# Layer 0 of the first two groups ahead of the branch, the search in 16 parts on two engines, and weights of layers 2 and 3 prepared in a later stage

## The chip, the cores and the metric

The kernel runs on one core of one Trainium2 chip. The metric is the device time of one execution in microseconds; of several executions the median is given. The profile is one execution, recorded by the hardware profiler.

## What is computed

Four graph layers follow each other on x (128 batches of 128 tokens by 128 features) with one adjacency of 128 x 128 integers per batch. Before each layer stands h = relu(layernorm(x)), after it x = x + layer(h).

```python
# layer 0
for r in range(1, 8):
    mask = (adj == r); degree = clip(mask.sum(2), 1e-6)
    agg += ((mask / degree) @ h) @ rel_weights[r]
out = relu(layernorm(agg + h @ self_w.T + self_b) * gamma + beta)
# layer 1
D = abs(h[:, :, None, :] - h[:, None, :, :])     # all pairs of tokens
s = leaky(batchnorm(D @ W1.T + b1)) @ W2 + b2    # one score per pair
A = softmax(where(adj > 0, s, -9e15))
y = leaky(batchnorm((A @ h) @ Wg.T + bg)); out = [h, y] @ Wt.T + bt
# layers 2 and 3: graph attention with weights W_2, b_2, a_2 and W_3, a_3
```

The inputs hold an adjacency of zeros and ones only, so relations 2 to 7 never occur. The kernel doesn't assume that: it looks for the highest number in the adjacency and branches on it.

## The kernel before

**Groups and tiles.** The 128 batches are taken in groups of four (G = 4, so 32 groups, NG). A group's x, adj, mask and so on are tiles of 128 x 512. Each batch's pairs are cut into four tiles of 128 x 2048 (NT = 4), 512 tiles in all.

**Start (to L559).** Two groups (AHEAD = 2) begin layer 0 in the generators `layer0(g)`, which run up to `po` (L346 to L351) and stop there, since they lack the sum over the other relations. Beside them `highest` (L274) takes the whole adjacency (8 MB) through VectorE in eight parts of 1 MB, four loaded over ScalarE's queue and four over SP's, through four buffers, and forms `flag` (L391). Then the weights of layers 2 and 3 are prepared (L394 to L467: transposes, products, squares against a bound, a split of the bias into three bf16 pieces), the weights of layer 1 are loaded (L469 on), and the constant `both_t` is made (L505).

**Branch (L512 to L561).** With a flag the other relations are computed for all groups and put into AGG. Without one (`cmp.Else()`, the arm that runs here) the self bias is copied into AGG: two tiles on the chip for groups 0 and 1, and two DRAM tensors `a` of 1.5 and 6 MB for the other 30 groups, by two DMAs on SP (L559). Then both generators finish layer 0 of groups 0 and 1: add, layernorm, gamma and beta, add to x, store to X[g], moments, and H1[g] on ScalarE.

**The pairs stage (to L799).** All further work of layer 0 and of the pairs is a list of `step`s: a name, an engine, a cost, the steps it waits for, a rank and the code. `features` (xp, xe, again, pw, xw) prepares two batches, `pairs` has per tile the difference `d` (L585, tiles 1 and 3 of four on GpSimd, the others on VectorE), `abs` (L624, ScalarE), `hp` (L595, L598, TensorE), `hs` (L608, ScalarE) and `st` (L615, VectorE), and `chain(g)` is layer 0 of group g from 2 on (load, mask, mv, deg, rs, most, per, hn, share, pt, hT, ... o, mvo, rso, oc, on, end, x, mvx, rsx, h1). The load of a group (L685 to L687) is three DMAs on SP: x, adj, and its AGG, into two buffers each.

`_ordered` makes one order of these steps. It keeps a free time per engine and a done time per step; the step with the earliest possible start goes next, the rank decides among equal starts only. A step that waits for names that are not in the list counts as ready at time 0. A step on SP is done LANDING = 3.0 us after its cost:

```python
        done[name] = start + cost + (LANDING if engine == "SP" else 0)
```

The emission runs in a region in which each engine issues its instructions in the order in which they are written (`tc.manual_schedule()`). Instructions outside of such regions are ordered by the compiler, by readiness.

**Layer 1's second half (to L1080).** One slot per batch turns stored pair products into scores; `chain(g)` puts softmax and products of a group into slots 4g + 5 to 4g + 16 by `at(slot, place, work)`. In a slot the places come in the order am, e, p, a, l, s. The last batch has slot 127; in slots 128 to 140 only chains of the last groups are left. Then comes the branch on `bounded` (L1093), with layers 2 and 3 in its arm.

Of the kernel before, what the change touches and what calls it, by code (L numbers as in the profile page):

```python
# [17 lines left out]
P = 128  # L18
G = 4
# [13 lines left out]
AHEAD = 2  # L33
FETCHED = 10
# [132 lines left out]
def tile_gnn_stack(ctx: ExitStack, tc: tile.TileContext, a: dict, out: bass.AP):  # L167
# [89 lines left out]
    with tc.tile_pool(name="c0", bufs=1) as c0, tc.tile_pool(name="p0", bufs=2) as p0:  # L257

        both = c0.tile([P, 2, P], F32, name="both")
        nc.sync.dma_start(both[:, 0, :], a["rel_w"][1])  # L260
        nc.sync.dma_start(both[:, 1, :], a["self_wT"])
# [6 lines left out]

        AGG = [c0.tile([P, G, P], F32, name=f"agg{g}") for g in range(AHEAD)] + AGG
# [5 lines left out]

        def highest(sc):

            n = NB * P // 8
            tops = sc.tile([P, 8], F32, name="tops")
            flat = a["adj"].rearrange("b t s -> b (t s)").rearrange("b (c n) -> c b n", c=8)  # L280
            for c in range(8):
                part = sc.tile([P, n], I32, name="part", bufs=4)
                (nc.scalar if c < 4 else nc.sync).dma_start(part, flat[c])
                nc.vector.tensor_reduce(tops[:, c:c + 1], part, AX.X, OP.max)
            top = sc.tile([P, 1], F32, name="top")
            nc.vector.tensor_reduce(top, tops, AX.X, OP.max)
            pt = sm("ptop")
            nc.tensor.transpose(pt[0:1, 0, :], top, ident)
            nc.vector.tensor_reduce(top[0:1, :], pt[0:1, 0, :], AX.X, OP.max)
            return top[0:1, :]  # L290
# [8 lines left out]
        def act_norm(dst, src, rs, nb):  # L299

            for k in range(G):
                nc.scalar.activation(dst[:, k, :], src[:, k, :], AF.Relu, bias=nb[:, k:k + 1],
                                     scale=rs[:, k:k + 1])
# [4 lines left out]

        def layer0(g):
            bs = slice(g * G, g * G + G)  # L310
            x = p0.tile([P, G, P], F32, name="x")
            nc.sync.dma_start(x, a["x"][bs].rearrange("b t c -> t b c"))
            adj = p0.tile([P, G, P], I32, name="adj")
            nc.sync.dma_start(adj, a["adj"][bs].rearrange("b t s -> t b s"))
            yield
            mv = small.tile([P, G, 2], F32, name="lnmv")
            rs = small.tile([P, G], F32, name="lnrs")
            norm_stats(x, mv, rs)
            nb = shift(mv, rs)
            yield  # L320

            mask = p0.tile([P, G, P], F32, name="mask")
            nc.gpsimd.tensor_scalar(mask, adj, 1, None, op0=OP.is_equal)
            deg = small.tile([P, G], F32, name="deg")
            nc.vector.tensor_reduce(deg, mask, AX.X, OP.add)
            nc.vector.tensor_scalar(deg, deg, 1e-6, None, op0=OP.max)
            nc.vector.reciprocal(deg, deg)
            yield
            h = p0.tile([P, G, P], F32, name="hn")
            act_norm(h, x, rs, nb)  # L330
            nc.gpsimd.tensor_tensor(mask, mask, deg[:, :, None].to_broadcast([P, G, P]), OP.mult)
            nc.gpsimd.tensor_scalar(M8[g], adj, 0, None, op0=OP.is_gt)
            yield
            hT = p0.tile([P, G, P], F32, name="hT")
            transpose(hT, h)
            yield
            maskT = p0.tile([P, G, P], F32, name="maskT")
            transpose(maskT, mask)
            yield
            o = p0.tile([P, G, P], F32, name="o")  # L340
            hw = p0.tile([P, G, P], F32, name="hw")
            ph = sm("ph")
            for k in range(G):
                nc.tensor.matmul(ph[:, k, :], hT[:, k, :], both[:, 0, :], start=True, stop=True)
            nc.scalar.copy(hw, ph)
            yield  # L346
            po = sm("po")
            for k in range(G):
                nc.tensor.matmul(po[:, k, :], hT[:, k, :], both[:, 1, :], start=True, stop=False)
                nc.tensor.matmul(po[:, k, :], maskT[:, k, :], hw[:, k, :], start=False, stop=True)  # L350
            nc.vector.tensor_copy(o, po)  # L351
            yield "rest"
            nc.vector.tensor_tensor(o, o, AGG[g], OP.add)
            yield
            mv = small.tile([P, G, 2], F32, name="lnmv")
            rs = small.tile([P, G], F32, name="lnrs")
            norm_stats(o, mv, rs)
            yield
            for k in range(G):
                nc.vector.scalar_tensor_tensor(o[:, k, :], o[:, k, :], mv[:, k, 0:1], gamma,  # L360
                                               op0=OP.subtract, op1=OP.mult)
            yield
            on = sm("on")
            for k in range(G):
                nc.vector.scalar_tensor_tensor(on[:, k, :], o[:, k, :], rs[:, k:k + 1], beta,
                                               op0=OP.mult, op1=OP.add)
            nc.vector.scalar_tensor_tensor(x, on, 0.0, x, op0=OP.max, op1=OP.add)
            nc.sync.dma_start(X[g], x)
            yield
            norm_stats(x, MV1[:, g], RS1[:, g])  # L370
            nb = shift(MV1[:, g], RS1[:, g])
            yield
            H1[g] = p0.tile([P, G, P], F32, name="h1", bufs=3)
            act_norm(H1[g], x, RS1[:, g], nb)


        H1 = {}
        first = [layer0(g) for g in range(AHEAD)]
        for w in first:
            next(w)  # L380
        with tc.tile_pool(name="sc", bufs=1) as sc:
            top = highest(sc)
            flag = const.tile([1, 1], I32, name="flag")
            for t, v in ((gamma, "gamma"), (beta, "beta")):
                nc.vector.tensor_copy(t, load(v, [P, P], _bcast(a[v], P), pool=c0))
            for k in range(G):
                nc.sync.dma_start(selfb[:, k, :], _bcast(a["self_b"], P))
            for w in first:
                while next(w) != "rest":
                    pass  # L390
            nc.vector.tensor_scalar(flag, top, 1.5, None, op0=OP.is_gt)  # L391

        with tc.tile_pool(name="sw", bufs=1) as sw:


            w2x = const.tile([P, P + 8], F32, name="w2x")
            nc.sync.dma_start(w2x[:, 0:P], a["W_2"])
            w3x = const.tile([P, P + 2], F32, name="w3x")
            nc.sync.dma_start(w3x[:, 0:P], a["W_3"])
            b_2 = load("b_2", [P, P], _bcast(a["b_2"], P))  # L400
            b_2c = col("b_2c", a["b_2"])
            wtyT = load("wtyT", [P, P], a["WtT"][P:2 * P])
            a2 = const.tile([P, 2, 4], F32, name="a2")
            nc.vector.memset(a2, 0.0)
            a3 = const.tile([P, 2, 1], F32, name="a3")
            for part in range(2):
                for hd in range(4):

                    nc.sync.dma_start(a2[32 * hd:32 * hd + 32, part, hd:hd + 1], a["a_2"][32 * (1 - part):][0:32])
                nc.sync.dma_start(a3[:, part, :], a["a_3"][P * (1 - part):][0:P])  # L410
            add_b = sw.tile([P, 8], F32, name="add_b")
            bounds = sw.tile([P, 3, 8], F32, name="bounds")
            nc.vector.memset(bounds, 0.0)
            square = sw.tile([P, 10], F32, name="square")
            for wx, av, n in ((w2x, a2, 4), (w3x, a3, 1)):
                pt = sm("pwt")
                nc.tensor.transpose(pt[:, 0, :], wx[:, 0:P], ident)
                wt = sw.tile([P, P], F32, name=f"wt{n}")
                nc.scalar.copy(wt, pt[:, 0, :])
                pv = sm("pwa")  # L420
                nc.tensor.matmul(pv[:, 0, 0:2 * n], wt, av.rearrange("p a b -> p (a b)"), start=True, stop=True)
                nc.vector.tensor_copy(wx[:, P:], pv[:, 0, 0:2 * n])
                nc.vector.tensor_tensor(square[:, 0:2 * n], wx[:, P:], wx[:, P:], OP.mult)
                pn = sm("pn")
                nc.tensor.matmul(pn[:, 0, 0:2 * n], ones, square[:, 0:2 * n], start=True, stop=True)
                nc.vector.tensor_copy(bounds[:, 0 if n == 4 else 1, 0:2 * n], pn[:, 0, 0:2 * n])
# [82 lines left out]
        for hh in range(2):  # L509
            nc.vector.tensor_tensor(fold[:, hh, :], ident[:, 0:64], ident[:, 64:128], OP.add)  # L510
# [1059 lines left out]
```

## Time and profile before

| | |
|---|---|
| median of 3 runs | 2887.32 us (2887.09 to 2894.89) |
| the profiled execution | 2891.87 us, of which its span 2889.8 |
| mean granted TensorE clock | 0.952 |
| busy: TensorE, VectorE, ScalarE, GpSimd | 85%, 87%, 83%, 60% |
| start, up to the first difference of pairs | 0 to 80 us |
| pairs stage | 80 to about 1600 us |
| layer 1's second half | about 1610 to 2411 us |
| layers 2 and 3 | 2414 us to the end |

How to read it: times are from the span's start. In the timeline a line is start, duration, engine, line of the kernel, operation, output and input tile and how often it comes in a row; in brackets stands how long the engine was idle before, and who ended that. A `q` behind an engine's name is its instruction queue, where DMAs are issued. In the chain of waits each line is a link of the path that ended last.

### The profile page before, as it was taken

To read this page: it belongs to the slowest core of one execution; us is meant where nothing else is said; L and a number is where in the kernel's file an instruction comes from. 1 tells how busy PE (TensorE), PEld (TensorE's weight loads), DVE (VectorE), ACT (ScalarE), POOL (GpSimd) and SP (SyncE) were. 2 spreads that over 40 slices of the span, in tenths; PEclk is the share of its full clock that TensorE was granted. 3 is DMA by queue.
4 is the path that set the end of the run, shared out by engine and by line. 5 is a ranking of instruction groups with operands and counts; after the bars stand their busy time and mean duration, and the time that the engine had idled before them with its cause. 6 is when DMAs were issued, how large, how long until landed. Compare 5 with 4: busy or idle time off the path is not lost.

```text
span 2889.8 us, 41921 instructions
## 1 busy us (share of the span) xinstructions
PE 2469.7 (85%) x14517; PEld 1185.7 (41%) x14517; DVE 2520.0 (87%) x4949; ACT 2392.2 (83%) x2811; POOL 1729.1 (60%) x1613
## 2 busy tenths in 40 slices
PE   1899899999898989898989688888888886998897
PEld 1333333333333333333333234444444444777675
DVE  5799999999999999999999578888888885987886
ACT  1799998989899999999999678777877774988886
POOL 2899989898989899898988001101111104665552
PEclk8899999999999999999999899999999997999998
DMA  5555545454544444454544999999999971111210
GB/s 200 201 202 221 204 190 204 190 204 190 204 193 200 195 199 200 193 207 186 215 171 204 368 408 408 410 409 409 410 410 410 408 283 54 45 59 63 63 34 27
DMA packets 180083, 653.83 MB, mean 226 GB/s; under 512 B 30992, under 2 KB 99472, under 8 KB 129680
## 3 DMA queue, kind: packets, MB, share of 16 engines
q1 hardware_dynamic: 179280, 646.80, 56.3%
q10 hardware_dynamic: 576, 4.19, 0.4%
q8 instruction: 119, 1.95, 0.3%
q14 instruction: 108, 0.88, 0.1%
HBM read 338.14 MB, written 312.80 MB: 225 GB/s over the span
## 4 chain that ended last, share of the span: by engine, by line
PE 36%; ACT 23%; DMA 20%; DVE 12%; issue 5%; POOL 3%; SPq 0%; DVEq 0%; ACTq 0%; POOLq 0%
PE hp L595 17%; ACT d L624 11%; DMA z<-hp 7%; DMA rows<-sk 7%; PE hp L598 5%; ACT hs L608 5%; DMA u<-rows 5%; DVE d L585 3%; PE pv L1292 2%; ACT o L717 2%; PE ps L919 1%; ACT h L1176 1%; DVE z L962 1%; PE po L741 1%; POOL rs L221 1%
## 5 line engine op out<-in xcount | busy, mean ns | idle before, releaser
L585 POOL TENSOR_TENSOR d<-xe 128x2048 f32<-128x2048 f32 x256 | 1074.0, 4201 | 86.2 <-PE hp L595 65.7
L595 PE MATMUL hp<-d,w1T 128*64 128x512 f32 x4096 | 1019.2, 621 | 123.1 <-ACT d L624 65.4
L624 ACT ACTIVATE d<-d 128x2048 f32<-128x2048 f32 x384 | 730.9, 1922 | 9.2 <-POOL d L585 5.0
L585 DVE TENSOR_TENSOR d<-xe,xp 128x2048 f32<-128x2048 f32 x256 | 579.9, 2265 | 28.6 <-PE xp L660 21.2
L608 ACT COPY hs<-hp 128x1024 f32<-128x1024 f32 x512 | 512.1, 1017 | 80.2 <-PE hp L598 43.3
L595 PEld LDWEIGHTS hp<-d,w1T 128*64 128x64 f32 x4096 | 290.9, 142 | 691.7 <-issue 465.3
L1008 POOL TENSOR_TENSOR x<-x,bt 128x512 f32<-128x512 f32 x32 | 43.7, 1366 | 684.7 <-DMA x<-x 684.7
L615 DVE BATCH_NORM_STATS2 st<-hs 128x6 f32<-128x512 f32 x512 | 348.8, 681 | 51.6 <-ACT hs L608 51.6
L616 DVE BATCH_NORM_STATS2 st<-hs 128x6 f32<-128x512 f32 (+1 forms) x512 | 328.7, 642 | 0.0
L962 DVE SCALAR_TENSOR_TENSOR z<-z 128x2048 f32<-128x2048 f32 x128 | 297.0, 2320 | 22.8 <-ACT z L944 22.8
L944 ACT ACTIVATE z<-z,bias,scale 128x2048 f32<-128x2048 f32 x128 | 267.3, 2088 | 18.8 <-DMA z<-hp 18.8
L948 ACT ACTIVATE zr<-z,bias,scale 128x2048 f32<-128x2048 f32 x128 | 267.4, 2089 | 9.7 <-DMA z<-hp 7.5
L598 PE MATMUL hp<-both_t,xw 128*64 128x512 f32 x1024 | 266.2, 594 | 0.0
L919 PE MATMUL ps<-z,w2z 128*32 128x512 f32 x1024 | 141.7, 626 | 83.2 <-DVE z L962 83.2
L926 PEld LDWEIGHTS pk<-pick,su 128*128 128x128 f32 x1024 | 125.7, 193 | 139.9 <-DVE su L940 103.0
L926 PE MATMUL pk<-pick,su 128*128 128x16 f32 x1024 | 138.2, 267 | 25.8 <-DVE su L940 24.7
L1292 PE MATMUL pv<-wr,e 128*128 128x128 f32 x1024 | 148.4, 293 | 10.7 <-DVE e L1269 6.1
L1292 PEld LDWEIGHTS pv<-wr,e 128*128 128x128 f32 x1024 | 133.8, 204 | 19.7 <-issue 3.8
L919 PE MATMUL ps<-z,w2l 128*32 128x512 f32 x1024 | 139.1, 612 | 0.6 <-DMA z<-hp 0.6
L919 PE MATMUL ps<-zr,w2r 128*32 128x512 f32 x1024 | 139.0, 615 | 0.4 <-ACT zr L948 0.4
L598 PEld LDWEIGHTS hp<-both_t,xw 128*64 128x64 f32 x1024 | 78.1, 138 | 143.1 <-issue 142.5
L1269 DVE SCALAR_TENSOR_TENSOR e<-e,ps 128x512 f32<-128x512 f32 x160 | 106.8, 678 | 28.7 <-ACT ps L1266 27.9
(266 smaller groups left out, 3855.5 us busy)
## 6 DMA issues: line engine op xcount, KB each, us to landing
hp<-hs SPq DMA_DIRECT2D x128, 2048.0 KB, 6.3
z<-hp SPq DMA_DIRECT2D x256, 1024.0 KB, 14.8
x<-x SPq DMA_DIRECT2D x128, 256.0 KB, 4.8
u<-rows SPq DMA_DIRECT2D x32, 384.0 KB, 11.6
x<-in_x_dram SPq DMA_DIRECT2D x32, 256.0 KB, 3.0
adj<-in_adj_dram SPq DMA_DIRECT2D x32, 256.0 KB, 3.4
out_dram<-x SPq DMA_DIRECT2D x32, 256.0 KB, 2.5
agg<-a SPq DMA_DIRECT2D x30, 256.0 KB, 3.8
```

What stands on the lines that cost most here:

```text
L585: eng.tensor_tensor(d, ahead, x[:, None, None, :].to_broadcast([P, 2, KC, P]), OP.max if t == BY_MAX else OP.subtract)
L595: nc.tensor.matmul(hp[64 * hh:64 * hh + 64, c:c + 512], w1T2 if by_max else w1T, d[:, hh, c:c + 512], start=True, stop=not by_max, skip_gr ...
L598: nc.tensor.matmul(hp[64 * hh:64 * hh + 64, c:c + 512], XW[i // NT // 2][:, i // NT % 2, :], both_t.rearrange("p h k i -> p h (k i)")[:, h ...
L608: nc.scalar.copy(halves[b][:, t, :], linear.pop(i))
L615: nc.vector.bn_stats(st[:, 2 * t, :], hs[:, 0:512])
L616: nc.vector.bn_stats(st[:, 2 * t + 1, :], hs[:, 512:1024 - P * last])
L624: nc.scalar.activation(diffs[i], diffs[i], AF.Abs)
L919: nc.tensor.matmul(ps[32 * c:32 * c + 32, :], w[:, w0:w0 + 32], v[:, 512 * c:512 * c + 512], start=j0 == 0, stop=w is w2r, skip_group_chec ...
L944: nc.scalar.activation(z0, z0, AF.Identity, bias=bias1, scale=scale1[:, 0:1])
L948: nc.scalar.activation(zr, z1, AF.Relu, bias=bias1, scale=scale1[:, 0:1])
L962: nc.vector.scalar_tensor_tensor(z0, z0, 0.01, z0, op0=OP.mult, op1=OP.max)
L1292: nc.tensor.matmul(t[pv][:, k % 2, hd, :], t[e][:, hd, :], flat[:, at:at + P], start=True, stop=True)
```

## The change

`layer0` and `highest` are gone. The functions `difference` to `features` and `chain` stand earlier in the code, otherwise as they were, but for three things: `chain` takes an `agg` that is already on the chip, its step `ph` waits for `first_loads` too, and its step `on` for `banks`. The start is now a list of steps with its own `_ordered` plan: layer 0 of groups 0 and 1 whole, with the self bias as `agg`, and the search, in 16 parts of 0.5 MB through eight buffers, all loaded on SP, even parts by a maximum on VectorE and odd ones by a sum of relu(adj - 1) on ScalarE.

```diff
-        first = [layer0(g) for g in range(AHEAD)]
...
+        step("first_loads", "SP", 3.0, [("load", AHEAD - 1)], 0, first_loads)
+        step("second_loads", "SP", 1.5, [("part", PARTS // 2 - 1)], 0, second_loads)
+        for c in range(PARTS):
+            step(("part", c), "SP", 1.25 * 16 / PARTS,
+                 ["first_loads"] if c == 0 else [("part", c - 1)] + [("top", c - PARTS // 2)] * (c >= PARTS // 2)
+                 + ["second_loads"] * (c == PARTS // 2), 1, lambda c=c: part(c))
+            step(("top", c), "ACT" if c % 2 else "DVE", 1.2 * 16 / PARTS, [("part", c)], -99, lambda c=c: highest(c))
+        step("top", "DVE", 0.4, [("top", c) for c in range(PARTS)], -99, highest_of_all)
+        step("ptop", "PE", 0.3, ["top"], -99, one_row, takes=("sm",))
+        step("flag", "DVE", 0.4, ["ptop"], -99, flagged, gives=("sm",))
+        step("banks", "ACT", 0.6, ["second_loads"], -40, in_banks)
+        step("both_t", "DVE", 2.6, ["second_loads"], 99, both_tokens)
+        step("fold", "Pool", 0.5, [], 99, folds)
+        for g in range(AHEAD):
+            chain(g, selfb)
+        with tc.manual_schedule():
+            for work in _ordered(steps, {"sm": 2}):
+                work()
```

`first_loads` holds self bias (four DMAs) and both weights of layer 0, `second_loads` gamma, beta and w1T; `banks` copies gamma and beta into PSUM; `both_t` makes w1T2, turns and both_t.

In the branch, the arm with a flag runs `chain(g, o)` for groups 0 and 1 once more with the true sum; the other arm only has the two DMAs into `a`. Behind the branch, the load of group 2 is taken out of the plan and issued first, outside of the hand-written order, and about 30 loads of weights of layers 1 to 3 follow it:

```diff
+        next(s for s in steps if s[0] == ("load", AHEAD))[-1]()
+        steps[:] = [s for s in steps if s[0] != ("load", AHEAD)]
+        b1 = col("b1", a["b1"], 64)
...
+        w2x = const.tile([P, P + 8], F32, name="w2x")
+        nc.sync.dma_start(w2x[:, 0:P], a["W_2"])
...
+                nc.sync.dma_start(a2[32 * hd:32 * hd + 32, part, hd:hd + 1], a["a_2"][32 * (1 - part):][0:32])
```

The preparation of the weights of layers 2 and 3 becomes `brief()`, placed into the last slots of layer 1's second half (end = NB + 1 = 129), behind the chains' own jobs of the same place:

```diff
+            at(end, "a", scratch)
+            at(end, "p", transposed)
+            at(end + 1, "am", copied)
+            at(end + 1, "p", products)
+            at(end + 2, "l", squares)
+            at(end + 3, "p", sums)
+            at(end + 4, "l", compared)
+            at(end + 1, "l", joined)
+            for n in range(3):
+                at(end + 5 + n, "l", lambda n=n: piece(n))
+            at(end + 8, "l", owners)
```

`pick` is now one copy on GpSimd instead of sixteen on VectorE, `fold` is made on GpSimd, and some memsets moved there.

## The prediction

> **What bounds the kernel now.** I read the slices first, then the timeline and the DMA issues of the first 110 us, then the chain at the end of layer 1. Of the 40 slices (72.2 us each) only a few show a hungry TensorE: the first, and the stretch around the seam of layers 1 and 2. The change touches these two places.
>
> ```profile
> PE   1899899999898989898989688888888886998897
> PEclk8899999999999999999999899999999997999998
> DMA  5555545454544444454544999999999971111210
> ```
>
> In the first slice TensorE is busy one tenth: all engines wait for the branch (L512). Its timeline:
>
> ```profile
> 24.27 2.29 DVE L284 TENSOR_REDUCE tops<-part 128x1 f32<-128x2048 int32 x1 [6.76 <-DMA part<-in_adj_dram]
> ...
> 41.45 0.14 DVE L391 TENSOR_SCALAR flag<-top 1x1 int32<-1x1 f32 x1
> ...
> 60.80 1.30 SPq L559 DMA_DIRECT2D a<-selfb  x2
> ...
> 71.56 5.29 SPq L368 DMA_DIRECT2D x<-x  x2
> ...
> 80.41 8.34 POOL L585 TENSOR_TENSOR d<-xe 128x2048 f32<-128x2048 f32 x2
> 81.24 2.29 DVE L585 TENSOR_TENSOR d<-xe,xp 128x2048 f32<-128x2048 f32 x1 [6.25 <-PE xp L660]
> ...
> 84.33 0.40 SPq L685 DMA_DIRECT2D x<-in_x_dram  x1
> ...
> 87.18 0.87 DVE L694 BATCH_NORM_STATS2 lnst<-x 128x6 f32<-128x128 f32 x4 [1.02 <-DMA x<-in_x_dram]
> ```
>
> The flag is there at 41.6, weights work keeps the branch until 58.2 (SP), the rest of layer 0 of groups 0 and 1 fills 63 to 80, and the first differences `d` start at 80.4 (GpSimd) and 81.2 (VectorE). From there about 3 us a tile. The DMA issues of that window, size and median time to landing:
>
> ```profile
> a<-selfb SPq DMA_DIRECT2D x1, 6144.0 KB, 21.7
> ...
> x<-x SPq DMA_DIRECT2D x2, 256.0 KB, 11.0
> ```
>
> The second line is the one to keep: X[0]'s store, issued at 71.56, let the load behind it go only at 84.2, just after the 6 MB of `a` had landed (61.6 + 21.7 = 83.3). Small transfers issued on SP behind that write end with it.
>
> **What the Trainium skill says.** "DMA: Bandwidth & Descriptors", section "Queues, rings and completion order": SP owns one ring on each of the DMA engines and descriptors are consumed in ring order; the 11.0 us of the stores agree (all issues of that name have a median of 4.8 over the run). "TensorE: Matmul & The Clock Gate", section "What's actually happening": half clock after idling, full after sustained work; the trace has a granted clock of 0.50 from 58 to 84 us and 0.58 from 80 to 90, so both kernels enter the pairs cold. "Runtime: NRT & Kernel Launch", section "Instruction fetch mechanics": a taken branch out of the fetched window stalls; here SP needed 2.6 us from branch (58.2) to first DMA (60.8).
>
> **The change, part by part.**
>
> *Search.* `part(c)` names `part(c-1)` as predecessor, and the planner adds LANDING 3.0 to every SP step; so it spaces the parts 1.25 + 3.0 = 4.25 apart: part 7 due at 41.2, the second loads at 45.4, parts 8 and 9 at 49.9 and 54.2. `both_t` and `banks` wait for the second loads (49.9), so `end(0)` is due at 53.9 and the store X[0] at 55.4: ahead of part 10. X[1] (59.7) comes ahead of part 11. A queue is in order: parts 10 to 15 can't leave before layer 0 of these groups is stored. In before the manual orders were kept literally (VectorE ran d, d, mv(2), mv(3), d, as planned), so I take this one literally too.
>
> *Layer 0 of groups 0, 1, ahead of the flag.* x lands at about 4 (3.0 from issue). GpSimd paces it: mask 1.50, roots with shift 1.95, `most` 0.2, m8 1.50, share 1.04 a group: share(0) at 10.9, share(1) at 17.2. Then transposes 0.6, maskT 0.6, `ph` 1.1, hw 0.6, `po` 1.9: `po(1)` ends at 22.6; o 0.7 and moments 1.2: 24.6; roots 1.95: 26.6; centring 1.65: 28.3. ScalarE has top 3, 5, 7 queued next (1.1 each, from 1.92 for twice the elements and 1.02 for a copy of this size) and `banks` 0.55: 32.1. VectorE meanwhile did top 2, 4, 6 (1.14, half of 2.28) and both_t 2.8. on(0) 1.35 and end(0) 0.68: 34.1; top 8 1.14, moments 1.16, on(1), end(1): 38.4. Then SP sends X[1] and parts 11 to 15. A lone 1 MB part took 5.2, of which 2.6 is transfer at 400 GB/s; a half one is 3.9, the store 0.65, each further part 1.3: part 15 at 39.0 + 0.65 + 3.9 + 5.2 = 48.7. top 15 1.1, closing steps 1.2 as before: flag at about **51**. That is 9 later than before, but with nothing left in front of the branch.
>
> *Branch.* Flag read 0.7 and branch 2.6: the `a` writes leave at 54.4 instead of 60.8.
>
> *Load of group 2, moved behind them.* `load(AHEAD)` is taken from the plan, so the planner holds mv(2) and mask(2) ready at time 0 and puts them first on VectorE and GpSimd, ahead of `again(0)`, `d(1)`, `deg(2)`, `d(0)`. Queued behind them is the whole pair work. Their x lands 84.2 - 60.8 = 23.4 after the write's issue: 77.8, adj 0.65 later: 78.5. mask 1.5, `again` 0.3: d(1) at 80.4. deg 0.67: d(0) at 80.8. Against 80.4 and 81.2: **-0.2**. The 26 us that the earlier layer 0 would give are spent in this wait; `features` (xp, xe, pw, xw, some 2 us) hides in it.
>
> *Ramp.* Before, mv(2), mv(3), mask(2), deg(2) stood between the first differences, with waits of 1.0 and 2.6 for x; d(6) began at 95.98. Now only mv(3) does, and its x, issued after the weights, lands near 85. d(6) follows hp(2), near 94: **-2**. The 30 weight DMAs (0.43 each, 13 us of SP) lie in SP's idle time, as `out(0)` is not due until 20 us into the pairs; with that cover gone they cost 13.
>
> *Weights for layers 2, 3 in the tail.* The removed 7.6 us (51.6 to 59.2) lay before the branch and are counted above. `brief` runs in slots 129 to 137, where the last two groups go alone:
>
> ```profile
> 2397.22 0.70 DVE e L1016
> 2398.01 0.70 DVE e L1017
> 2398.73 0.70 DVE mx L1022
> 2399.45 0.70 DVE e L1023
> 2400.18 0.64 ACT e L1062
> 2400.84 0.70 DVE sums L1027
> ```
>
> This chain has no gaps, so what stands between its links costs in full: transposes and b_2c product on PE in slot 129 0.9, `joined` 0.3 (slot 130), `squares` 0.6 (131), `piece` 0 and 1 0.75 each (134, 135) by the durations of L417 to L441. What falls in slots 132, 133, 136, 137 meets an idle VectorE. **+3.3**; between +1 (if PE's and half of VectorE's hide) and +6 (if the three more `sm` banks make a product wait).
>
> *Small edits.* `pick` in one GpSimd copy, `fold` on GpSimd, memsets: under 1 us each, hidden by the search.
>
> Sum: -0.2 - 2 + 3.3 = **+1.1**. Against the profiled execution: 2891.87 + 1.1 = 2893.0; it lies 4.55 above the median, so the median goes from 2887.32 to about **2888**. Unknown: ScalarE's accumulating Relu on int32 is not in the trace; at 0.9 to 1.5 the seven of them that count move the flag by -1 to +3. Own range of this case 2882 to 2895.
>
> **Rivals.**
>
> *Loads leave ahead of the branch (faster).* Work not in a hand-written order can move up a queue: SP's own read of `bounded`, written far below, ran ahead of its branch.
>
> ```profile
> L512 SPq COMPARE_BRANCH  x1: 50/50/50, 58.2 to 58.2; - x1
> ```
>
> ```profile
> L1093 SPq TENSOR_LOAD <-bounded x1: 285/285/285, 57.6 to 57.6; - x1
> ```
>
> x's first buffer is free at about 41. If x and adj of group 2 go then, VectorE starts d(0) near 57, but mv(3) comes third, and its x still ends with the `a` write, at 78.5: d(4) ends at 82 instead of 94.3, so -12.4 + 3.3: **2878**. If group 3's go too, d(0) at 57 instead of 81.2, -24 + 3.3 and most of the ramp's 2: **2867**. Against it: the branch's other arm uses the same buffers, and must find them free.
>
> *Flag later (slower).* From 51 on each us of flag is a us of time, since wait and write hang on it. The 30 weight loads wait for nothing; if they sit on SP ahead of parts 10 to 15, after X[0] or X[1], instead of in the gap before part 8, they add 13 us there, less 2 to 3 by loads gone from the ramp: **2898**. It decides from a flag after 59. For it: w3x needed 5.0 us of SP[...].
>
> **How the numbers follow.** As forecast 0.45; group 2 early 0.15; groups 2 and 3 early 0.17; flag later 0.23. About 0.3% (8.7 us) is what a measurement can tell from no change. Faster: 0.17, half of the 2878 case, 0.05 of the forecast's spread: 0.30. Slower: 0.21 of the late flag and 0.03: 0.24. Same: 0.46. The range 2866 to 2899 takes in the rivals' values and leaves out their outer halves, below 0.2.
>
> **What would show it.** Right: X[1]'s store ahead of part 11 on SP; flag at 48 to 55; VectorE's first work after the branch is moments of x with a wait near 20 us on DMA x; d(1) near 80; the tail after the last `ps` longer by 2 to 4. Wrong: x of group 2 issued before the branch; a flag before 40 (stores not in front of parts) or after 59; parts spread by weight loads.

## The result and the profile after

| | before | after |
|---|---|---|
| median | 2888.2 us (2887.09 to 2894.89, 4 runs) | 2893.7 us (2890.22 to 2897.68, 4 runs) |
| ratio after / before, 95% interval | | 1.0017, 1.0000 to 1.0034 |
| profiled execution, its span, TensorE clock | 2891.87, 2889.8, 0.952 | 2892.36, 2890.5, 0.946 |

The time hardly moved, and what difference there is lies on the slow side. Layer 0 of two groups and the weights of layers 2 and 3 are no longer behind the search, and nothing came of it. In the slices of the page after, the first one is a little fuller for TensorE, 2 in place of 1, and the second, in which the pairs begin, is emptier, 6 in place of 8.

```profile
PE   2699998989898999898989688888888886998897
PEclk7899999999999999999999799999999997999998
DMA  6445444444445454544444899999999971111210
```

The timeline of the kernel after, from the flag to the third pair of differences (start, duration, engine, line, operation; in brackets the idle time before it and who ended it):

```profile
54.68 0.14 DVE L562 TENSOR_SCALAR flag<-top 1x1 int32<-1x1 f32 x1
...
58.99 1.74 SPq L659 DMA_DIRECT2D a<-selfb  x2
61.54 12.48 SPq L700 DMA_DIRECT2D a<-in_a_dram  x1
...
75.41 1.18 SPq L411 DMA_DIRECT2D agg<-a  x1
76.69 1.19 SPq L408 DMA_DIRECT2D x<-in_x_dram  x1
82.69 0.37 SPq L409 DMA_DIRECT2D adj<-in_adj_dram  x1
...
84.79 0.87 DVE L420 BATCH_NORM_STATS2 lnst<-x 128x6 f32<-128x128 f32 x4 [29.97 <-DMA x<-in_x_dram]
86.45 1.50 POOL L430 TENSOR_SCALAR mask<-adj 128x512 f32<-128x512 int32 x1 [41.42 <-DMA adj<-in_adj_dram]
88.27 8.33 POOL L308 TENSOR_TENSOR d<-xe 128x2048 f32<-128x2048 f32 x2
88.59 4.48 DVE L308 TENSOR_TENSOR d<-xe,xp 128x2048 f32<-128x2048 f32 x2
96.14 2.29 DVE L308 TENSOR_TENSOR d<-xe,xp 128x2048 f32<-128x2048 f32 x1 [2.02 <-PE hp L318]
```

Four things are to be seen. VectorE and GpSimd stand still for 30 and 41 us (the first part of that is still the wait for the flag and the branch), and what ends both waits is the load of group 2. That load isn't late by its own size: SP sends x 17.7 us after the first of the two writes of `a`. Right behind the writes stands a load of 128 bytes for a_2, in whose issue SP is held for 12.48 us. And adj leaves 6 us after x, because SP waits before it. The DMA issues of the first 110 us have the write, and the waits of SP have that wait (who waited, for what, us in total, how often, longest):

```profile
a<-selfb SPq DMA_DIRECT2D x1, 6144.0 KB, 22.9
...
x<-in_x_dram SPq DMA_DIRECT2D x4, 256.0 KB, 4.1
```

```profile
SPq L409 <- DMA a<-selfb: 4.8, 1, 4.8
```

The 6 MB write, issued at 59.74, had landed at 82.6, and adj (L409) left at 82.69. So the write holds the load of group 2 in two ways: x by its place in the queue, adj by a wait for the write's landing.

Cut at marks that both kernels have, the spans differ so (in brackets the mark in the trace after):

| stretch | before | after | difference |
|---|---|---|---|
| to the first `d` on GpSimd (88.27) | 80.41 | 88.27 | +7.86 |
| to the end of the pairs stage, the memset of `zero` (1611.77) | 1527.52 | 1523.50 | -4.02 |
| to the end of the last product `ps` (2379.15) | 768.55 | 767.38 | -1.17 |
| to the moments at the seam of layers 1 and 2 (2416.14) | 34.76 | 36.99 | +2.23 |
| layers 2 and 3, to the end | 478.56 | 474.36 | -4.20 |
| sum | 2889.8 | 2890.5 | +0.7 |

The last row is not laid to the change: the code of that stage is the same in all kernels, the ten kernels below took between 472.7 and 477.7 there, and from 120 to 240 us after the seam the granted clock was 0.94 and 0.91 (60 us each) in the profiled execution before, 0.97 in both after. The first, second and fourth rows make +6.1, and the medians differ by 5.5.

### The profile page after: what moved, and what is told of

Read it like the earlier page. It is cut to its first block, busy times and chain, and to the rows that moved or that the text cites. A ratio compares the mean times of both kernels' runs of the same rounds, so it can differ in the third digit from the quotient of the medians.

```text
span 2890.5 us, 41926 instructions
## 1 busy us (share of the span) xinstructions
PE 2472.1 (86%) x14515; PEld 1187.6 (41%) x14515; DVE 2504.7 (87%) x4905; ACT 2403.4 (83%) x2838; POOL 1730.3 (60%) x1628
## 4 chain that ended last, share of the span: by engine, by line
PE 35%; ACT 23%; DMA 19%; DVE 12%; issue 5%; POOL 4%; SPq 0%; DVEq 0%; ACTq 0%; POOLq 0%
PE hp L318 16%; ACT d L347 10%; DMA z<-hp 7%; DMA rows<-sk 6%; ACT hs L331 5%; DMA u<-rows 5%; PE hp L321 5%; DVE d L308 3%; PE pv L1300 2%; PE ps L830 2%; POOL d L308 2%; ACT o L443 1%; ACT h L1184 1%; DVE z L873 1%; PE po L467 1%
## 5 line engine op out<-in xcount | busy, mean ns | idle before, releaser
L347 ACT ACTIVATE d<-d 128x2048 f32<-128x2048 f32 x384 | 730.9, 1922 | 37.1 <-POOL d L308 35.0
L308 DVE TENSOR_TENSOR d<-xe,xp 128x2048 f32<-128x2048 f32 x256 | 579.7, 2265 | 26.5 <-PE xp L383 15.6
L1277 DVE SCALAR_TENSOR_TENSOR e<-e,ps 128x512 f32<-128x512 f32 x160 | 106.8, 678 | 28.6 <-ACT ps L1274 27.8
```

Of the source, the lines that this page charges most:

```text
L308: eng.tensor_tensor(d, ahead, x[:, None, None, :].to_broadcast([P, 2, KC, P]), OP.max if t == BY_MAX else OP.subtract)
L347: nc.scalar.activation(diffs[i], diffs[i], AF.Abs)
```

## The experiments

The theory after this comparison: the start is bounded by the load of group 2, which is queued on SP behind the `a` writes; everything that the change wins ahead of it is waited away. The rival: the flag, which came 13 us later than before, is what counts. A third reason, for the tail, is that `brief` sits between the links of the last chains.

| kernel | median | ratio to before, 95% interval | first `d` on GpSimd | memset of `zero` |
|---|---|---|---|---|
| load in order | 2891.19 | 1.0010 (1.0001 to 1.0019) | 85.50 | 1608.80 |
| writes on ScalarE's queue | 2881.84 | 0.9974 (0.9967 to 0.9982) | 74.80 | 1596.28 |
| parts unchained | 2890.08 | 1.0006 (0.9998 to 1.0014) | 83.97 | 1607.62 |
| load in the plan | 2886.23 | 0.9992 (0.9984 to 1.0000) | 59.73 | 1601.06 |
| tail moved | 2887.89 | 1.0001 (0.9992 to 1.0009) | 88.22 | 1610.34 |
| early loads | 2869.26 | 0.9936 (0.9922 to 0.9949) | 60.99 | 1584.00 |
| early loads, parts unchained | 2876.25 | 0.9957 (0.9944 to 0.9971) | 48.18 | 1591.53 |
| the same, writes and tail moved | 2861.22 | 0.9910 (0.9895 to 0.9926) | 53.25 | 1583.86 |
| early loads in the plan, parts unchained | 2857.11 | 0.9882 (0.9864 to 0.9900) | 50.42 | 1573.83 |
| the same, writes and tail moved | 2855.95 | 0.9879 (0.9862 to 0.9895) | 53.41 | 1577.29 |

**The load in the order of the code.** It is issued in a hand-ordered region of its own.

```diff
-        next(s for s in steps if s[0] == ("load", AHEAD))[-1]()
+        with tc.manual_schedule():
+            next(s for s in steps if s[0] == ("load", AHEAD))[-1]()
```

> One edit to the kernel after: the load of group 2 is put into a hand-written order, so that its x and adj leave SP ahead of its AGG. Theory (the first differences wait for x and adj of group 2, and these end with the 6 MB write of a that stands before them): x and adj can't pass the write, so only what SP lost by its own order comes back: the first difference on GpSimd goes from 88.3 to about 85, the median from 2893.7 to about 2891. Rival (the wait is made by the order of SP's queue, not by the write): x lands within 5 us of the write's issue, the first difference is at about 66, and the median falls by some 18.

d(1) came at 85.50, 2.8 earlier, as expected, but only half of this is the order: the flag came 1.2 earlier in this run and the writes 1.4 (57.59), though nothing ahead of them was edited. (In the six kernels with this start the flag came between 52.8 and 55.2.) From the write to d(1) it is 27.9 us in place of 29.3. One a_2 load still stood behind the write and held SP for 12.65 us; only the load of AGG fell behind x and adj. So the order among the small loads is worth 1.4 us, and the rest is the write.

**The writes on another queue.** As the last one, and:

```diff
-                nc.sync.dma_start(t.rearrange("p n g t -> p n (g t)"),
+                nc.scalar.dma_start(t.rearrange("p n g t -> p n (g t)"),
```

> As e1_order, and the two writes of a are issued on ScalarE's queue instead of SP's. Theory (x and adj wait in SP's rings behind the write): in rings of its own the write shares the engines with the loads; x and adj land 4 to 8 us after their issue, first difference at 66 to 70 instead of 88, median about 2893.7 - 20 = 2874. Rival one (the engines are busy with the write, whichever ring it is in): first difference stays near 85, median 2891. Rival two (the start is held by the branch, features and the cold TensorE, so that what the wait gives back is lost a few tiles later): first difference early, but the first store of hp, at 105.9 after, moves by less than 5.

The timeline and, under it, the issues and two of SP's waits of this kernel:

```profile
57.06 1.71 ACTq L659 DMA_DIRECT2D a<-selfb  x2
...
59.35 1.42 SPq L408 DMA_DIRECT2D x<-in_x_dram  x1
64.61 0.37 SPq L409 DMA_DIRECT2D adj<-in_adj_dram  x1
...
68.76 0.87 DVE L420 BATCH_NORM_STATS2 lnst<-x 128x6 f32<-128x128 f32 x4 [15.92 <-DMA x<-in_x_dram]
...
72.97 1.50 POOL L430 TENSOR_SCALAR mask<-adj 128x512 f32<-128x512 int32 x1 [29.52 <-DMA adj<-in_adj_dram]
```

```profile
a<-selfb ACTq DMA_DIRECT2D x1, 6144.0 KB, 23.6
```

```profile
SPq L411 <- DMA a<-selfb: 16.4, 1, 16.4
...
SPq L409 <- DMA a<-selfb: 3.8, 1, 3.8
```

The write is as long as ever, and x lands in the midst of it, 9.4 us after its issue. So it was the place in SP's queue that held x, not the bytes alone. This agrees with the Trainium skill ("DMA: Bandwidth & Descriptors", section "Queues, rings and completion order"): SP and ScalarE own a queue each, and a DMA engine takes from the queues in turn, packet by packet. The direction was as expected, the size was not: d(1) at 74.8, where 66 to 70 was expected. x took 9.4 us beside the 6 MB, and adj left 5.3 us after x. For 3.8 of these SP waited, and it went on at 64.61, when the 1.5 MB write of `a` (issued at 57.06, 7.5 us to landing) was there; the load of AGG behind adj waited 16.4 us, until the 6 MB had landed at 81.4. So the other queue frees the loads from the place behind the write, but SP is still held by its landing. The gain isn't lost later, as rival two had it: the first store of hp went from 105.9 after to 91.4. Against the last run it is 9.35 us in the median.

**The parts unchained.** The parts have no predecessor but the buffer that they need.

```diff
-                 ["first_loads"] if c == 0 else [("part", c - 1)] + [("top", c - PARTS // 2)] * (c >= PARTS // 2)
-                 + ["second_loads"] * (c == PARTS // 2), 1, lambda c=c: part(c))
+                 [("top", c - PARTS // 2)] * (c >= PARTS // 2), 1 + c / 100, lambda c=c: part(c))
```

> One edit to the kernel after: a part of the search no longer names the part before it, so the planner doesn't count 3 us of landing between two parts, and all 16 stand ahead of the stores X[0] and X[1] in SP's queue. Theory (the flag is late because ten parts' worth of search stood behind the two stores): the last part lands by about 32, the flag is there at 34 to 40, and SP reaches the branch after X[1] at about 45; writes of a at 47 instead of 59, first difference 12 earlier at about 76, median about 2882. Rival (the search is bound by its transfers, or the chain is slowed by the searches ahead of it on VectorE and ScalarE as much as the flag gains): X[1]'s store moves from 41.8 to 50 or later, and the median changes by less than 4.

This was meant as the test of the rival, that the flag decides. The flag came at 39.9, 14.9 us earlier, as early as before the change; d(1) came 4.3 earlier and the time hardly changed. Its timeline on SP:

```profile
44.03 0.48 SPq L683 DMA_DIRECT2D w2z<-in_W_dram  x1
49.08 1.29 SPq L658 DMA_DIRECT2D a<-selfb  x2
50.85 12.81 SPq L684 DMA_DIRECT2D w2z<-in_W_dram  x1
...
78.18 0.40 SPq L408 DMA_DIRECT2D x<-in_x_dram  x1
78.68 0.45 SPq L409 DMA_DIRECT2D adj<-in_adj_dram  x1
```

The writes left 9.9 us earlier, x 1.5 us later than after the change. With parts tightly packed on SP, only 13 of the 30 weight loads stood ahead of the branch, and SP was busy with them until 44.5, 4.6 us past the flag. The other 17 came to stand between the write and x, the first of them held for 12.81 us. I had expected 2882, and left this out: the loads that wait for nothing had filled the gaps between the parts, and with the gaps closed they went to the next place, here the worst one. So in this kernel the early flag is worth next to nothing, but the run doesn't show what it would be worth with the order of the loads unchanged; two things moved at once.

**The load in the plan.** The planner is left an empty step ("load", 2), so it doesn't take moments and mask of group 2 for ready at time 0.

```diff
-        steps[:] = [s for s in steps if s[0] != ("load", AHEAD)]
+        steps[:] = [s[:-1] + (lambda: None,) if s[0] == ("load", AHEAD) else s for s in steps]
```

> One edit to the kernel after: the load of group 2 stays in the plan as a step without work, so the planner knows that mv(2) and mask(2) come later and puts them behind the first differences. The write and the loads are untouched. Theory (mv(2) and mask(2) stand first in VectorE's and GpSimd's queues and hold all pair work): first difference at about 62; then mv(2) waits as the third piece of VectorE to 85, so d(4) starts at about 88 instead of 96.1: median about 2893.7 - 7 = 2887. Rival (the first differences were held by something else, as the branch or TensorE): first difference still near 88, no change.

GpSimd's timeline:

```profile
59.73 8.34 POOL L308 TENSOR_TENSOR d<-xe 128x2048 f32<-128x2048 f32 x2
84.04 1.50 POOL L430 TENSOR_SCALAR mask<-adj 128x512 f32<-128x512 int32 x1 [15.96 <-DMA adj<-in_adj_dram]
```

Four differences now run before the wait, at once after `xe`, and the wait for adj shrinks from 41 to 16 us. That saves what the place of moments and mask in the queues cost, 7.5 us of the median (7 were expected), and the load is nearly as late as ever (x left SP at 75.48). This shows directly that the first `d` was ready near 60 and queued behind mask(2).

**The tail moved.** Each job of `brief` is put into a slot in which its engine is idle.

```diff
-            at(end, "p", transposed)
-            at(end + 1, "am", copied)
-            at(end + 1, "p", products)
-            at(end + 2, "l", squares)
-            at(end + 3, "p", sums)
-            at(end + 4, "l", compared)
-            at(end + 1, "l", joined)
+            at(end + 2, "p", transposed)
+            at(end + 3, "am", copied)
+            at(end + 3, "p", products)
+            at(end + 4, "l", squares)
+            at(end + 5, "p", sums)
+            at(end + 7, "l", compared)
+            at(end + 3, "l", joined)
...
-                at(end + 5 + n, "l", lambda n=n: piece(n))
+                at(end + 4 + n // 2 * 3, "l", lambda n=n: piece(n))
```

> The preparation of the weights of layers 2 and 3 is moved, job by job, into slots or places where the last chains leave the engines idle (transposes in slot 131, copies and products 132, squares and the split 133, sums 134, the comparison 136, pieces 133 and 136). Nothing else differs from the changed kernel. Theory: the 2.2 us by which the seam of layers 1 and 2 came later, beyond what the start cost, is these jobs standing between the chains' links; here they fall into gaps, so from the last product to the seam it takes about 2 us less, 2891.7 in all. Rival: it is the number of jobs and not their place, or something else in the tail; then the seam stays where it was, within 0.5 us, and the time within 1 of 2893.7.

VectorE between the comparison with `cap` and the maximum of a chain, in the kernel after:

```profile
2401.58 0.69 DVE L928 TENSOR_TENSOR e<-e,cap 128x512 f32<-128x512 f32 x1
2402.19 0.21 DVE L1051 CAST brief<-brief 3x136 bf16<-3x136 f32 x1
2402.44 0.29 DVE L1052 TENSOR_TENSOR brief<-brief 3x136 f32<-3x136 f32 x1
2402.66 0.34 DVE L1053 SCALAR_TENSOR_TENSOR brief<-brief,ident 3x136 f32<-3x136 bf16 x1
2402.93 0.67 DVE L933 TENSOR_REDUCE mx<-e 128x4 f32<-128x512 f32 x1
```

and in this one:

```profile
2399.82 0.69 DVE L928 TENSOR_TENSOR e<-e,cap 128x512 f32<-128x512 f32 x1
2400.54 0.69 DVE L933 TENSOR_REDUCE mx<-e 128x4 f32<-128x512 f32 x1
```

From one link to the next it is 1.35 us in the first and 0.72 in the second. From the end of the last `ps` to the seam it takes 35.20 us, against 36.99 after and 34.76 before: 1.8 of the 2.2 us are given back by place alone. All eleven kernels with the change bear this out: the eight with the jobs in their first place take 37.0 to 38.1 us there, the three with them moved 35.2 to 35.9. The medians of separate batches of runs (2887.89 and 2893.7) differ by more, but the intervals of both ratios meet, so I take the size from the trace.

**The loads of groups 2 and 3 ahead of the branch.**

```diff
+        first = {}
+
+        def fetch(t, g, x, adj, pool):
+            bs = slice(g * G, g * G + G)
+            t["x"] = pool.tile([P, G, P], F32, name=x)
+            nc.sync.dma_start(t["x"], a["x"][bs].rearrange("b t c -> t b c"))
+            t["adj"] = pool.tile([P, G, P], I32, name=adj)
+            nc.sync.dma_start(t["adj"], a["adj"][bs].rearrange("b t s -> t b s"))
...
+        with tc.manual_schedule():
+            ea = ctx0.enter_context(tc.tile_pool(name="ea", bufs=1))
+            for g in (AHEAD, AHEAD + 1):
+                t = {}
+                fetch(t, g, f"x_{g}", f"adj_{g}", ea)
+                first[g] = t["x"], t["adj"]
...
-        next(s for s in steps if s[0] == ("load", AHEAD))[-1]()
-        steps[:] = [s for s in steps if s[0] != ("load", AHEAD)]
```

> x and adjacency of groups 2 and 3 are loaded into buffers of their own right behind the last part of the search, ahead of the branch; the load of group 2 stays in the plan and has only the copy of its self bias left. The writes stay on SP, the parts as they were. Theory: after the flag (still near 55) nothing but the features stands in front of the pairs, so the first difference on GpSimd starts near 61 instead of 88, and no difference waits for moments of a late x: 24 to 27 us less, 2868. Rival: the pairs start at 61 too, but the plan's loads of self bias and the first stores of products then wait on SP behind the 6 MB, and the stall only comes some tiles later, as in the run with the load in the plan (d stalled from 68 to 84): 2882 or more.

The waits of this kernel between 45 and 92 us, in which no x or adj appears any more, and GpSimd's first difference:

```profile
POOL xe L392 <- ACT xe L379: 16.0, 1, 16.0
PEld hp L318 <- issue: 9.5, 29, 1.3
DVE d L308 <- PE xp L383: 8.0, 1, 8.0
```

```profile
60.99 4.17 POOL L308 TENSOR_TENSOR d<-xe 128x2048 f32<-128x2048 f32 x1
```

The theory's 2868 was met with 2869.26, and the pairs stage ended 27.8 us earlier than after the change. The AGG loads left SP only at 76.2 and 77.5 us, and the first store of products waited 5.5 us for the landing of the write, but nothing needed them so early; the rival's second stall didn't come. This settles the main question: the gain of the changed start was spent, to within a few us, in the wait for the loads of groups 2 and 3.

**The earlier flag on top of it.** Early loads, and the parts unchained as above.

> As the kernel with early loads of groups 2 and 3, and the parts of the search without a predecessor, so that they leave as their buffers come free (flag near 45 in the run that did this alone). Theory: with no load to wait for, all of the earlier flag is time: the first difference near 48, 12 us less than with early loads alone, 2856. Rival: the weights, which the earlier parts push behind the branch and behind the 6 MB write, hold up the stores of products and the next loads on SP, and the gain is 4 as in the run of parts alone: 2864.

It missed both values: 2876.25, slower than early loads alone. The timeline:

```profile
40.40 0.14 DVE L573 TENSOR_SCALAR flag<-top 1x1 int32<-1x1 f32 x1
...
49.54 1.29 SPq L675 DMA_DIRECT2D a<-selfb  x2
51.43 12.68 SPq L401 DMA_DIRECT2D x<-in_x_dram  x1
...
74.16 0.87 DVE L431 BATCH_NORM_STATS2 lnst<-x 128x6 f32<-128x128 f32 x4 [20.22 <-DMA x<-in_x_dram]
```

d(0) and d(1) did start at 49, but the loads of x and adj, placed only by a region of their own, stood behind the 6 MB write again (L401 after L675). Why the compiler put them there in this kernel and not in the last one I have not found out. The same with the writes on ScalarE's queue and the tail moved:

> As the last one, with the writes of the self bias on ScalarE's queue and the weights' preparation moved in the tail. Theory: the tail gives 2 us, the other queue lets weights and loads pass the 6 MB and is worth 0 to 2 us: 2853. Rival: the stores and loads of the first tiles were what held the pairs, and then the queue alone brings 8 or more: 2846. If ScalarE's issuing of the two writes delays the features, the first difference starts 2 us later and the time is 2857.

2861.22: it missed all three values, which were reckoned from 2856, but it is 15 us less than the run before it. Of these, 7.7 are there at the memset of `zero` and 2.9 are the tail's, from the last `ps` to the seam; the rest is spread over stages with the same code. So where loads stand behind the write, the queue is worth some 8 us. adj of group 3 still left SP only at 55.9, GpSimd's third difference came at 65.5, and behind that SP waited 16.6 us for the landing of the write, though it was on the other queue. This makes a bad place for the loads less costly; the next run gives them a fixed one.

**The early loads as a step of the plan.** As early loads with unchained parts, but (the parts from 7 on then wait for `("top", c - 7)`):

```diff
-            found[c] = search.tile([P, n_part], I32, name="part", bufs=PARTS // 2)
+            found[c] = search.tile([P, n_part], I32, name="part", bufs=7)
...
+        def fetched():
+            for g in (AHEAD, AHEAD + 1):
+                t = {}
+                fetch(t, g, f"x_{g}", f"adj_{g}", c0)
+                first[g] = t["x"], t["adj"]
+
+        step("early", "SP", 2.0, [("part", 6)], 1.065, fetched)
```

> As the run with early loads and unchained parts, but the four loads of groups 2 and 3 are a step of the first plan, behind part 6, so that their place ahead of the branch is fixed; for their room the search has seven buffers instead of eight. Theory: that run lost because its four loads had slipped behind the 6 MB write (x left SP at 51 to 67, and VectorE waited 20.2 us for it). With their place fixed, the early flag (40.5 there) counts: first difference at 50 to 51, 10 to 11 us ahead of the run with early loads alone and no stall after it, 2859. Rival: the weights behind the 6 MB write are what costs in that run, by holding the first stores of products and the loads of self bias until 83 to 88; then tiles from about the twelfth on wait for a free buffer of products and the time is 2870 or more.

```profile
49.79 1.30 SPq L676 DMA_DIRECT2D a<-selfb  x2
50.42 8.34 POOL L308 TENSOR_TENSOR d<-xe 128x2048 f32<-128x2048 f32 x2
...
51.63 13.88 SPq L699 DMA_DIRECT2D w2z<-in_W_dram  x1
...
58.72 1.51 POOL L441 TENSOR_SCALAR mask<-adj 128x512 f32<-128x512 int32 x1
61.22 4.19 POOL L308 TENSOR_TENSOR d<-xe 128x2048 f32<-128x2048 f32 x1 [0.98 <-PE hp L318]
```

The flag came at 42.1, 1.6 later than with the loads behind the write, weights are held behind the write as there, and it takes 2857.11 us, 19 less. The weights cost nothing that shows, so the rival falls: the 10.6 us by which the first difference is ahead of that of early loads alone are still 10.2 at the memset of `zero`. The earlier flag (11.7 us), worth next to nothing in the third run, is now worth 10 us in the trace and 12 in the median. With writes and tail moved as well:

> As the last one, with the writes of the self bias on ScalarE's queue and the weights' preparation moved in the tail. Theory: the tail's 2 us only, since nothing waits for SP any more: 2857. Rival: SP behind the write still holds weights and stores, and its release is worth 4 or more: 2853 or less.

2855.95, the best here, 1.2% under the kernel before (0.9879, 0.9862 to 0.9895), but not told apart from the last one by its interval. From the last `ps` to the seam it is 1.2 us shorter (35.9 against 37.1), and the first `d` is 3.0 later, since the flag was 1.7 later in this run and the two writes take 1.5 us of ScalarE's queue ahead of `xe`. Moving the write buys nothing here. It doesn't test the rival, though, since SP was not released:

```profile
SPq L705 <- DMA a<-selfb: 16.9, 1, 16.9
```

SP waited for the landing of the write ahead of the load of w3x, which left at 74.45, where it had left at 73.11 with the write on SP.

## Why the prediction came out, and where it did not

- **Value and range.** 2888 was forecast, 2882 to 2895 as the range of this case; it came to 2893.7, near the upper end.
- **Bound and mechanism.** Right. That "the 26 us that the earlier layer 0 would give are spent in this wait" is what the early loads show: with the wait gone, 2869 in place of 2894. The order on SP was as worked out from the planner: X[0]'s store (37.63) ahead of part 10 (38.01), X[1]'s (41.84) ahead of parts 11 to 15, and moments and mask of group 2 first in their queues.
- **Flag, 51.** It came at 54.8. Part 15, the closing steps and the accumulating Relu (1.14 us and 0.19 for the reading of its sum; I had 1.1) were sized about right. The step that failed is "GpSimd paces it", with `po(1)` at 22.6 (the terms given add up to 22.0). GpSimd ran as forecast (share(1) ended at 17.7, forecast 17.2), but TensorE waited for `both`, one of the first loads, until 15.64, a wait that the sum put at nothing although `ph` names `first_loads`:

```profile
15.64 2.05 PE L461 MATMUL ph<-both,hT 128*128 128x128 f32 x8 [3.19 <-DMA both<-in_rel_w_dram]
```

  `both` took 10.7 us from issue to landing, where the same load took 4.9 in the kernel before; why, no run shows. hw(0) waited for that product, and hn(1) is queued behind hw(0) on ScalarE (18.21), so `po(1)` ended at 26.2. Those 3.6 us ran on to `banks` and both `end`s (3.4 to 3.5 late each), to X[1]'s store and so to the last parts.
- **Writes, 54.4.** They left at 59.0: 3.8 by the flag, 0.8 because the branch took 4.2 us from the flag and not 3.4.
- **x landed at 77.8, d(1) at 80.4 (-0.2).** It was 84.8 and 88.27 (+7.86). Of the 8 us, 4.6 are those of the write. 2.4 come from x itself, which landed 25.8 us after the writes' issue where I took 23.4 from the kernel before. About half of that is the write: from the issue of the first to the landing of the second it took 23.7 us, before 22.5. The rest fits the a_2, a_3 and AGG loads, which went ahead of x here, while before X[0]'s store was the first thing behind the write; with AGG behind x, 0.6 came back. 1.0 is adj, which I put 0.65 behind x and which came 1.66 behind, since SP waited for the write's landing before it issued adj. I had the compiler's order wrong: 28 of the 30 weight loads, which I put behind the branch in SP's idle time, went ahead of it into gaps between the parts without delaying one, and the two that were left went ahead of x.
- **Ramp, -2.** Right in kind, -4.0: with features done since 63 us and only mv(3) between the first differences, they ran closer together than I allowed. d(6) began 12.2 us after d(1) (100.44), before 15.6 (95.98): 3.4 less, where I had 2.
- **Tail, +3.3.** Right in place, +2.23; the run that moved the jobs gives 1.8 of it back.
- **Sum, +1.1.** By these terms it was 7.86 - 4.02 + 2.23 = +6.1; the medians say +5.5. The start came 8 us later than forecast; 3 of these were taken back by a ramp and a tail that were better than forecast, which is luck, not foresight. The late flag was my second rival, with weight loads as its cause and 59 as the point where it decides. The flag missed that point, and its cause was another: what the weights did was stand ahead of x, not ahead of the parts. The first rival, loads ahead of the branch, didn't happen by itself; made by hand, it gave 2869 where I had 2867 (d(0) came at 61.8 and not at 57, so that the two are so near is in part chance).

## What to carry to other kernels

When work is moved ahead of a wait, ask first what the next instruction behind that wait needs, and where in which queue its load stands: here 25 us were won and waited away for loads of 256 KB behind a 6 MB write, and the cure was to send the load ahead. Another queue for the write was worth less, since SP went on to wait for its landing a few DMAs later. Loads that wait for nothing and weren't placed by hand took the gaps in their queue here, and closing the gaps pushed them into a worse place; what must not slip belongs into the plan, as a step. Value an edit in its context: 12 to 15 us of flag were worth next to nothing where they pushed loads ahead of the one that mattered, and 10 to 12 us once that load had its fixed place ahead of the branch.

## What the runs showed of the hardware

- The load next on SP behind the 6 MB write was held in its issue for 11.8 to 13.9 us in all eight kernels in which one stands right behind it (12.48 for a_2, 12.81 for w2z, 12.68 for x), and SP with it. With the write on ScalarE's queue the same a_2 load, issued 0.9 us after the write, took SP 0.33 us.
- In all eleven kernels with the change the fifth DMA issued after the 6 MB write left SP within 0.1 us of the write's landing, whichever of the two queues the write was on: adj at 82.69 in the kernel after (landing 82.6), AGG at 81.43 in the first with the write on ScalarE's queue (81.4), w3x at 74.45 in the last one (74.4). In that first one the fifth DMA after the 1.5 MB write was held in the same way (adj at 64.61, landing 64.6). The four in between were issued before. Whether the compiler or the chip sets this count, no run shows.
- From the memset of `zero` to the last `ps`, layer 1's second half took 767.1 to 769.7 us in all twelve kernels. Its DMA engines are busy throughout: in the windows' view of the kernel after, the columns are the stretch, its length, the busy time of TensorE, its weight loads, VectorE, ScalarE and GpSimd, the granted clock, the share of the DMA engines and GB/s.

```profile
1610.00:2375.00 765.00, 656.43 (x4942) 308.13 (x4946) 631.35 (x957) 597.11 (x402) 84.27 (x65) 0.96 1.01 403
```

  The length of this stage doesn't follow the start, which differs by up to 38 us between these kernels; what the start wins passes through it unchanged.
